# A gather attention kernel: the order of its tiles, the place of a scatter, and an early table load

## The chip, the cores and the metric

The kernel runs on one core of one Trainium2 chip. The metric is the device time of one execution in microseconds (us), lower is better. The core's engines are named as the profile names them: PE is TensorE's matmul stream and PEld its weight loads, DVE is VectorE, ACT is ScalarE, POOL is GpSimd, SP is SyncE. [...]Here POOL issues every indirect DMA (gathers and scatters of rows).

## The reference, cut to what matters

A graph attention layer with a layer norm ahead of it and a residual. N = 3327 nodes, 1024 features. The adjacency matrix is sparse and holds its diagonal; a row has between one and some 37 neighbours.

```python
h = jnp.maximum(_layernorm(x, axis=-1), 0.0)
f = h @ Wf + bf
g = h @ Wg + bg
e = jax.nn.relu(f @ g.T)
scores = jnp.where(adj > 0, e, -9.0e15)
attention = jax.nn.softmax(scores, axis=1)
x = x + attention @ (h @ W + bW)
```

## The kernel before, in words

**First part, 0 to some 258 us.** Rows of `adj` and `x` are read in 26 blocks of 128. For every row the kernel finds its neighbours' numbers (24 in the table `pd`, all candidates in the table `cd`), writes the normalized row to the table `hd`, and builds the product matrix `A_sb` out of Wf and Wg, so that one projection `q = h A` gives what a row is multiplied with. Then it ranks the rows by degree and writes the permutation `perm`.

**Second part, to the end.** The rows in the order of degree make 26 tiles of 128 rows. Tile `s` has `CAPS[s]` slots, one for each neighbour that its fullest row can have: 37, 25, 23, ... down to 11. The list `ORDER` says in which order the tiles are worked on; before, it is 24, 0, 1, ..., 23, 25. For a tile the steps are these:

- `fetch` gathers the neighbour lists `pi` and the tile's own rows (into a buffer `G`) on POOL.
- `prepare` transposes the own rows on PE (`hT`, L703, L704) and makes q on PE in three pieces of 342 columns (`ps_q`, L764); `emptied` and `prepared` copy q out on ACT. Tiles with `s < MORE` (0 and 1) can have more than 24 neighbours: `prepared` gathers their row of `cd` and finds the further numbers on DVE (`found`, `more`, L803 to L812).
- `dot` gathers one neighbour row of each of the 128 rows (512 KB, `G<-hd`, L691) and multiplies it with q on DVE (`junk`, L824).
- `softmax` works on the tile's scores on DVE and ACT.
- `combine` makes the weighted sum of the neighbour rows. A slot is either summed on DVE (`G`, L910), or scaled on ACT (L904) and summed by PE, as eight transposes that add up in `yT_ps` (L887). `on_tensor` chooses how many slots go to PE.
- `project` multiplies the sum with `W_sb` on PE (`ps_o`, L924).
- `result` copies that out on ACT to a tile `res`, and POOL adds the rows of x to it by a gather that accumulates (`res<-in_x_dram`).
- `finish` scatters `res` to the output on POOL (L954).

Tiles with more than 16 slots (`ONE_CHUNK`) are worked on in two units, for example tile 0 as slots 0 to 18 and 19 to 36; smaller ones in one unit, which is then also the last one. The main loop runs over the units. In the last unit of a tile it fetches the tile after next, combines, takes the `result` of the tile before, and prepares the tile after next. `project` of a tile with two-unit successor is put behind the combine of the successor's first unit (`rest`). The first three dots of the next unit (`AHEAD`) are put ahead of `combine`. There are 26 buffers `G`, which all the gathered rows share: a gather waits until the slot that used its buffer has been summed. The tile 24 that comes first has its 12 dots in thirds (`dots_of_first`, L842), and the second tile's gathers stand behind a small POOL copy (`gate`). A list scheduler keeps this order within an engine unless an instruction is not ready by its own estimate; `in_line` pins some of PE's and ACT's instructions to the written order.

Of the kernel before, what the change touches and what calls it, by code (L numbers as in the profile page):

```python
# [8 lines left out]
FP = mybir.dt.float32  # L9
I32 = mybir.dt.int32  # L10
AF = mybir.ActivationFunctionType
# [14 lines left out]

CAPS = [37, 25, 23, 22, 21, 21, 20, 20, 19, 19, 18, 18, 17, 17, 17, 16, 16, 15, 15, 15, 14, 14, 13, 13, 12, 11]

ORDER = [24, *range(24), 25]
ONE_CHUNK = 16  # L30
FIRST = 10
LARGEST = 16
# [263 lines left out]
def edge_path(ctx: ExitStack, tc: tile.TileContext, x, adj, Wf, bf, Wg, bg, W, bW, out, flag):  # L296
# [11 lines left out]
    nc = tc.nc  # L308
    N, D = x.shape
    O = W.shape[1]  # L310
    P = 128
# [26 lines left out]
    ident = const.tile([P, P], FP, name="ident")  # L338
# [345 lines left out]
    small = ctx.enter_context(tc.tile_pool(name="small", bufs=2))  # L684
# [5 lines left out]
    def gather(to, table, idx, **kw):  # L690
        return nc.gpsimd.indirect_dma_start(  # L691
            out=to,
            out_offset=None,
            in_=table,
            in_offset=bass.IndirectOffsetOnAxis(ap=idx, axis=0),
            **kw,
        )
# [13 lines left out]
    @contextmanager  # L711
    def in_line():
        with ExitStack() as both:
            for ins in queue.values():
                both.enter_context(tc.issue_after(ins.ins))
            yield
# [4 lines left out]
    def filled(pool, name, row, w, at):  # L721
        ps = pool.tile([P, CB], FP, name=name)
        if at < 2:
            nc.tensor.matmul(ps, ident, A_sb[:, 0, :CB], start=True, stop=True)
        o = at * w % row.shape[1]
        banks[name, at] = ps
        return nc.scalar.copy(ps[:, :w], row[:, o : o + w])

    for at in range(2):
        filled(p_q, "ps_q", vb, QB, at)  # L730
        filled(p_o, "ps_o", bWb, CB, at)

    def fetch(s):

        if s == ORDER[1]:

            with tc.issue_after(st["gathered"].ins):
                return fetched(s)
        fetched(s)
# [8 lines left out]
    def prepare(s):  # L748
# [9 lines left out]
        for i, o in enumerate(range(0, QW, QB)):  # L758
            at = 3 * ORDER.index(s) + i
            ps = banks.pop(("ps_q", at))  # L760
# [15 lines left out]
    def emptied(s, i):  # L776
        e = st[s]
        at = 3 * ORDER.index(s) + i
        with in_line():
# [37 lines left out]
    def dot(s, k, behind=None):  # L817
        e = st[s]
        g = G[s, k] = gpool.tile([P, D], FP, name="G")
        with tc.issue_after(st["gate"].ins) if s == ORDER[1] else ExitStack():  # L820
            st["gathered"] = gather(g, hd[:, :], e["edges"][k])
# [27 lines left out]
    def softmax(s, k0, k1, last):  # L849

        e = st[s]
        sc = e["sc"][:, k0:k1]
        nc.vector.scalar_tensor_tensor(sc, sc, 0.0, e["mask"][:, k0:k1], op0=ALU.max, op1=ALU.add)
        nm = small.tile([P, 1], FP, name="nm")
        nc.vector.tensor_reduce(nm, sc, AX.X, ALU.max, negate=True)
        if k0:
            nc.vector.tensor_tensor(nm, nm, e["nm"], op=ALU.min)  # L857
        l = small.tile([P, 1], FP, name="l")
        with in_line():
            nc.scalar.activation(sc, sc, AF.Exp, bias=nm, accum_out=l)  # L860
        if k0:
            al = small.tile([P, 1], FP, name="al")
            nc.scalar.activation(al, e["nm"], AF.Exp, bias=nm, scale=-1.0)
            nc.vector.scalar_tensor_tensor(l, e["l"], al, l, op0=ALU.mult, op1=ALU.add)
        if last:
            rs = small.tile([P, 1], FP, name="rs")
            nc.vector.reciprocal(rs, l)
            if k0:
                nc.vector.tensor_tensor(al, al, rs, op=ALU.mult)
            nc.vector.tensor_scalar(sc, sc, rs, None, op0=ALU.mult)  # L870
        if k0:
            queue["act"] = nc.scalar.activation(e["y"], e["y"], AF.Copy, scale=al)
        e["nm"], e["l"] = nm, l

    def on_tensor(s, k0, k1):


        m = min(max(0, CAPS[s] - (7 if s in ORDER[-2:] else 12)), k1 - k0 - 2) if s != ORDER[0] else (k1 - k0) // 2
        ks = range(max(k0, 1), k1)
        return [k for i, k in enumerate(ks) if (i + 1) * m // len(ks) > i * m // len(ks)]  # L880

# [11 lines left out]
    def combine(s, k0, k1, last):  # L893
        e = st[s]
        if not k0:
            e["y"] = G[s, 0]
        y = e["y"]
        e["first"] = True
        pe = on_tensor(s, k0, k1) if last else []
        for k in range(k0, k1):  # L900
            p = e["sc"][:, k : k + 1]
            g = G[s, k]
            if k in pe:
                queue["act"] = nc.scalar.activation(g, g, AF.Copy, scale=p)  # L904
                queue["pe"] = sum_transposed(e, g, e["first"], False)
                e["first"] = False
            elif k == 0:
                queue["act"] = nc.scalar.activation(y, y, AF.Copy, scale=p)  # L908
            else:
                e["summed"] = nc.vector.scalar_tensor_tensor(y, g, p, y, op0=ALU.mult, op1=ALU.add)  # L910

    def project(s):
# [7 lines left out]
        for o in range(OH):  # L920
            ps = banks.pop(("ps_o", OH * ORDER.index(s) + o))
            with in_line():
# [8 lines left out]
    def result(s):  # L931

        e = st[s]
        r = e["r"] = xpool.tile([P, O], FP, name="res")
        for o in range(OH):
            to, ps = r[:, o * CB : (o + 1) * CB], e["o"][o]
            if s == NT - 1:
                nc.vector.tensor_tensor(to, ps, e["x"][:, o * CB : (o + 1) * CB], op=ALU.add)
                continue
            at = OH * ORDER.index(s) + o + 2  # L940
            with in_line():
                ins = nc.scalar.copy(to, ps)  # L942
                if at < OH * NT:
                    ins = filled(p_o, "ps_o", bWb, CB, at)
            queue["act"] = ins


        if s < NT - 1:
            gather(r, x[:, :], perm[:, s : s + 1], compute_op=ALU.add)

    def finish(s):

        with tc.issue_after(st["gathered"].ins):
            ins = nc.gpsimd.indirect_dma_start(  # L954
                out=out[:, :],
                out_offset=bass.IndirectOffsetOnAxis(ap=perm[:, s : s + 1] if s < N // P else final, axis=0),
                in_=st[s]["r"],
                in_offset=None,
                bounds_check=None if s < N // P else N - 1,
                oob_is_err=s < N // P,  # L960
            )
        tc.declare_no_dep(ins.ins, group="results", reason="other rows")
        tc.add_to_no_dep_group("results", ins.ins)

    def failed():

        worst = small.tile([P, 1], FP, name="bad")
        nc.vector.tensor_reduce(worst, bads, AX.X, ALU.max)
        onesf = small.tile([P, 1], FP, name="onesf")
        nc.vector.memset(onesf, 1.0)  # L970
        ps = p_t.tile([P, 4, P], FP, name="ps_t")[:, 0, :]
        nc.tensor.matmul(ps[0:1, 0:1], worst, onesf, start=True, stop=True)
        nc.vector.tensor_copy(flag[0:1, 0:1], ps[0:1, 0:1])
        return nc.values_load(flag[0:1, 0:1], min_val=0, max_val=1 << 20)
# [8 lines left out]
    def dots(s, ks):  # L983
        for k in ks:
            if (s, k) not in done:
                done.add((s, k))

                dot(s, k, st[ORDER[-2]].get("summed") if s == ORDER[-1] else None)
# [13 lines left out]
    rest, done_with = None, []  # L1002
    for i, (s, k0, k1) in enumerate(units):
        last = k1 == CAPS[s]
        at = ORDER.index(s)
        if last and at + 2 < NT:
            fetch(ORDER[at + 2])
        dots(s, range(k0, k1))
        softmax(s, k0, k1, last)
        if i + 1 < len(units):  # L1010
            s2, a, b = units[i + 1]
            dots(s2, range(a, min(b, a + AHEAD)))
        if done_with:
            finish(done_with.pop())
        combine(s, k0, k1, last)
        if rest:
            rest()
            rest = None
        if last:
            if at:  # L1020
                result(ORDER[at - 1])
                done_with.append(ORDER[at - 1])
            if at + 2 < NT:
                prepare(ORDER[at + 2])

            def rest(s=s, at=at):
                if at + 2 < NT:
                    prepared(ORDER[at + 2])
                project(s)

            if not at or i + 1 == len(units) or units[i + 1][2] == CAPS[units[i + 1][0]]:
                rest()
                rest = None
            if at + 2 == NT - 1:
                bad = failed()
# [43 lines left out]
```

## Time and profile before

| | us |
|---|---|
| median of 14 runs | 1326.61 (1323.48 to 1333.57) |
| the profiled execution, its time | 1328.31 |
| its span in the profile | 1326.6 |
| DVE busy | 1165.1 (88%) |
| PE busy | 1110.6 (84%) |
| POOL busy | 893.6 (67%) |
| ACT busy | 597.0 (45%) |

The profiled execution took 1.7 us more than its span, and its time is 1.7 us over the median. A busy share is a mean over stages that have different limits: DVE's 88% hold a first part in which it waits for others, and PE's 84% hold a stretch in which it has nothing to do. The stages have to be read one by one.

### The profile page before, as it was taken

The numbers are of one execution on the slowest core, as the hardware profiler recorded it, in microseconds if no ns is written. First come the engines' busy times: TensorE is split into PE (matmuls) and PEld (weight loads), VectorE is DVE, ScalarE is ACT, GpSimd is POOL, SyncE is SP. The second block draws the span as 40 slices with busy tenths as digits, with TensorE's granted clock in tenths as the row PEclk, the third lists the DMA queues.
The fourth block names the chain that finished last, engine by engine and source line by source line (L and its number), as shares of the span: only waits on it lengthen the run. The fifth ranks groups of instructions, "written<-read, shape, count | busy, mean of one in ns | idle before, by whom it ended". The sixth has DMA issues, their size and how long they took to land.

```text
span 1326.6 us, 14333 instructions
## 1 busy us (share of the span) xinstructions
PE 1110.6 (84%) x4448; PEld 701.4 (53%) x4448; DVE 1165.1 (88%) x2360; ACT 597.0 (45%) x940; POOL 893.6 (67%) x678
## 2 busy tenths in 40 slices
PE   2588897298239679899999998999999999999995
PEld 2355564065035547665665664666566555555553
DVE  4779899769977888999999999999989999998980
ACT  6779688224043516552454454334433333333350
POOL 6699889275656667777776776676656777766611
PEclk9989898699669799999999998999999999999998
DMA  9999996697468788988989889888887899888831
GB/s 357 335 355 378 391 369 219 240 338 293 168 190 301 253 291 272 295 308 301 310 283 327 306 310 320 290 278 296 285 287 233 286 288 291 274 258 295 262 108 50
DMA packets 101660, 374.46 MB, mean 282 GB/s; under 512 B 14731, under 2 KB 18474, under 8 KB 98247
## 3 DMA queue, kind: packets, MB, share of 16 engines
q0 software_dynamic: 79584, 286.77, 64.9%
q1 hardware_dynamic: 11004, 71.01, 14.0%
q10 hardware_dynamic: 10986, 15.67, 3.3%
q8 instruction: 37, 0.61, 0.2%
q14 instruction: 49, 0.40, 0.1%
HBM read 344.11 MB, written 29.30 MB: 281 GB/s over the span
## 4 chain that ended last, share of the span: by engine, by line
PE 29%; DVE 24%; issue 18%; POOL 10%; ACT 9%; DMA 9%; POOLq 0%; ACTq 0%; DVEq 0%; SPq 0%
PE ps_o L924 14%; PE ps_q L764 10%; DVE G L910 7%; ACT G L904 5%; DVE junk L824 5%; DVE cand L478 5%; POOL r L427 5%; DMA G<-hd,pi 5%; POOL G L691 5%; PE yT_ps L887 4%; DMA res<-in_x_dram,perm 2%; DVE junk L842 1%; DVE held L487 1%; DVE cand L489 1%; ACT r L420 1%
## 5 line engine op out<-in xcount | busy, mean ns | idle before, releaser
L691 POOL DMA_INDIRECT G<-hd,pi x454 | 535.0, 1178 | 199.7 <-issue 102.0
L824 DVE CUSTOM_DVE_ANT_0 junk<-G,q 128x1024 bf16<-128x1024 f32 x456 | 584.7, 1282 | 52.9 <-DMA G<-hd,pi 31.2
L924 PE MATMUL ps_o<-W_sb,yT 128*128 128x512 f32 x832 | 367.0, 599 | 21.9 <-ACT yT L918 21.9
L764 PE MATMUL ps_q<-A_sb,hT 128*128 128x342 f32 x1248 | 367.4, 453 | 9.6 <-ACT hT L704 9.6
L910 DVE SCALAR_TENSOR_TENSOR G<-G,sc 128x1024 f32<-128x1024 f32 x279 | 357.8, 1282 | 6.0 <-ACT G L908 5.2
L764 PEld LDWEIGHTS ps_q<-A_sb,hT 128*128 128x128 f32 x1248 | 234.6, 190 | 134.4 <-ACT hT L704 15.8
L924 PEld LDWEIGHTS ps_o<-W_sb,yT 128*128 128x128 f32 x832 | 156.1, 190 | 217.4 <-issue 189.4
L887 PE MATMUL yT_ps<-ident,G 128*128 128x128 f32 x1512 | 186.5, 281 | 78.4 <-ACT G L904 78.4
L887 PEld LDWEIGHTS yT_ps<-ident,G 128*128 128x128 f32 x1512 | 173.8, 144 | 106.5 <-ACT G L904 90.8
L427 POOL TENSOR_TENSOR r<-r,iotaj 128x1664 f32<-128x1664 f32 (+3 forms) x52 | 191.3, 3709 | 29.9 <-ACT r L420 29.9
L904 ACT ACTIVATE G<-G,sc 128x1024 f32<-128x1024 f32 x163 | 173.2, 1136 | 53.1 <-DVE sc L870 53.1
L780 ACT COPY q<-ps_q 128x342 f32<-128x342 f32 x78 | 34.6, 443 | 270.7 <-PE ps_q L764 270.7
L478 DVE MAX8 cand<-r 128x8 f32<-128x208 f32 (+2 forms) x416 | 121.8, 360 | 29.1 <-POOL r L427 29.1
L554 PE MATMUL ps_A<-WgT,WfT 128*128 128x342 f32 x432 | 139.1, 481 | 0.2 <-ACT WfT L535 0.2
L554 PEld LDWEIGHTS ps_A<-WgT,WfT 128*128 128x128 f32 x432 | 85.6, 203 | 59.8 <-issue 19.6
L420 ACT ACTIVATE r<-r 128x3327 f32<-128x3327 int32 (+4 forms) x28 | 77.8, 2780 | 1.4 <-ACT xt L464 0.5
L954 POOL DMA_INDIRECT out_dram<-res,perm x25 | 29.1, 1166 | 65.9 <-DMA res<-in_x_dram,perm 64.4
L860 ACT ACTIVATE sc<-sc,nm 128x10 f32<-128x10 f32 (+11 forms) x41 | 12.6, 308 | 126.4 <-DVE nm L857 115.1
L691 POOL DMA_INDIRECT res<-in_x_dram,perm x25 | 44.4, 1774 | 34.7 <-ACT res L942 29.8
L691 POOL DMA_INDIRECT pi<-pd,perm x26 | 29.9, 1148 | 39.9 <-issue 34.1
L942 ACT COPY res<-ps_o 128x512 f32<-128x512 f32 x50 | 28.7, 575 | 55.8 <-PE ps_o L924 55.8
L704 ACT COPY hT<-ps_t 128x512 f32<-128x512 f32 x52 | 28.0, 587 | 40.2 <-PE ps_t L703 40.1
(133 smaller groups left out, 683.3 us busy)
## 6 DMA issues: line engine op xcount, KB each, us to landing
r<-in_adj_dram SPq DMA_DIRECT2D x25, 1663.5 KB, 10.9
xt<-in_x_dram SPq DMA_DIRECT2D x25, 512.0 KB, 8.6
hd<-xt ACTq DMA_DIRECT2D x25, 512.0 KB, 8.4
G<-hd,pi POOLq DMA_INDIRECT x454, 6.1
wr<-in_L_gnn_Wg_dram SPq DMA_DIRECT2D x8, 512.0 KB, 5.9
wr<-in_L_gnn_Wf_dram SPq DMA_DIRECT2D x8, 512.0 KB, 8.4
W_sb<-in_L_gnn_W_dram SPq DMA_DIRECT2D x1, 4096.0 KB, 17.8
cd<-cand ACTq DMA_DIRECT2D x25, 64.0 KB, 8.5
```

The costliest lines, as they stand in the source:

```text
L420: nc.scalar.activation(r[:n, b:e], a[:n, b:e], AF.Sign, accum_out=to)
L427: nc.gpsimd.tensor_mul(r[:n, b:e], r[:n, b:e], iotaj[:n, : e - b])
L478: nc.vector.max(cand[:n, s * 8 : s * 8 + 8], r[:n, s * SW : min(N, (s + 1) * SW)])
L554: nc.tensor.matmul(ps[:, :QB], WfTs[c][:, k, :], WgT[:, k, o : o + QB], start=(k == 0), stop=(k == KD - 1))
L691: return nc.gpsimd.indirect_dma_start(out=to, out_offset=None, in_=table, in_offset=bass.IndirectOffsetOnAxis(ap=idx, axis=0), **kw,)
L764: ins = nc.tensor.matmul(ps[:, :QB], hT[:, k, :], A_sb[:, k, o : o + QB], start=False, stop=(k == KD - 1), skip_group_check=True,)
L780: ins = nc.scalar.copy(e["q"][:, i * QB : (i + 1) * QB], e["ps_q"][i][:, :QB])
L824: nc.vector.tensor_tensor_reduce(junk, g, e["q"][:, :D], 1.0, e["q"][:, D : D + 1], op0=ALU.mult, op1=ALU.add, accum_out=e["sc"][:, k : k ...
L887: ins = nc.tensor.matmul(e["yT"][:, c, :], g[:, c * P : (c + 1) * P], ident, is_transpose=True, start=(first and c % 4 == 0), stop=(last a ...
L904: queue["act"] = nc.scalar.activation(g, g, AF.Copy, scale=p)
L910: e["summed"] = nc.vector.scalar_tensor_tensor(y, g, p, y, op0=ALU.mult, op1=ALU.add)
L924: ins = nc.tensor.matmul(ps, yT[:, k, :], W_sb[:, k, o * CB : (o + 1) * CB], start=False, stop=(k == KD - 1), skip_group_check=True,)
```

## The change

Four edits. The tile 15, which has 16 slots, moves from the seventeenth place to the second; tile 0 with its 37 slots becomes third, and tile 1 fourth. The rule of `on_tensor` for the first tile (half of the slots on PE) holds for the second one too: 8 slots of tile 15 go to PE, where it was 4. The scatter of a finished tile (`finish`) is issued in the next last unit and no longer in the next unit of any kind; the two differ where a tile has two units. And an exponential of one column is put ahead of the first copies of the second part, so that ACT's exponential table is loaded there.

```diff
-ORDER = [24, *range(24), 25]
+ORDER = [24, 15, *range(15), *range(16, 24), 25]
...
+    one = small.tile([P, 1], FP, name="one")
+    nc.scalar.activation(one, ident[:, :1], AF.Exp)
+
     for at in range(2):
         filled(p_q, "ps_q", vb, QB, at)
         filled(p_o, "ps_o", bWb, CB, at)
...
     def on_tensor(s, k0, k1):
-        m = min(max(0, CAPS[s] - (7 if s in ORDER[-2:] else 12)), k1 - k0 - 2) if s != ORDER[0] else (k1 - k0) // 2
+        m = min(max(0, CAPS[s] - (7 if s in ORDER[-2:] else 12)), k1 - k0 - 2) if s not in ORDER[:2] else (k1 - k0) // 2
...
-        if done_with:
+        if done_with and last:
             finish(done_with.pop())
```

## The prediction

> **What bounds the kernel now.** I read the share by slices first, then the busy time by stretches of 40 us, then the chain of work that ended last, then the timeline around the places that the change touches. The second part starts at 258 us, and the slices say that its limit changes on the way:
>
> ```profile
> PE   2588897298239679899999998999999999999995
> DVE  4779899769977888999999999999989999998980
> ```
>
> PE has its hole at slice 11 (around 350 us) and is full from about slice 25; DVE is nearly full between. The stretches give numbers (columns: stretch, length, busy PE, PEld, DVE, ACT, POOL with counts, PE clock, DMA share, GB/s):
>
> ```profile
> 300.00:340.00 40.00, 36.21 (x144) 21.89 (x144) 38.72 (x56) 13.89 (x22) 18.42 (x18) 1.00 0.62 229
> 340.00:380.00 40.00, 0.00 (x0) 0.00 (x0) 36.80 (x49) 0.00 (x0) 26.83 (x16) 0.52 0.61 198
> 460.00:500.00 40.00, 31.02 (x103) 17.71 (x102) 32.58 (x49) 10.95 (x22) 27.49 (x23) 0.94 0.85 288
> 620.00:660.00 40.00, 35.90 (x161) 22.95 (x160) 39.65 (x62) 19.43 (x30) 29.04 (x26) 1.00 0.90 304
> 1020.00:1060.00 40.00, 39.09 (x149) 24.09 (x148) 39.37 (x55) 13.51 (x23) 29.90 (x24) 1.00 0.92 303
> ```
>
> From 340 to 380 us PE does nothing: it has made q and o for all that is ready, and tile 0's 37 slots occupy DVE until 384. From 386 to some 620 us both have gaps, to 960 us DVE is the limit, and from there the chain of waits lies on PE without a break:
>
> ```profile
> 1029.24 14.00 PE ps_o L924 x32
> 1043.24 3.49 PE yT_ps L887 x32
> 1047.85 14.08 PE ps_q L764 x48
> 1063.47 14.00 PE ps_o L924 x32
> ```
>
> So the early tiles cost DVE time, the late ones PE time. The third view is the timeline at the first scatter and at the table load:
>
> ```profile
> 405.83 1.59 POOL L691 DMA_INDIRECT res<-in_x_dram,perm  x1 [0.30 <-issue]
> 409.35 1.02 POOL L691 DMA_INDIRECT G<-hd,pi  x1 [0.30 <-issue]
> 414.49 0.99 POOL L954 DMA_INDIRECT out_dram<-res,perm  x1 [4.12 <-DMA res<-in_x_dram,perm]
> 415.73 1.32 DVE L824 CUSTOM_DVE_ANT_0 junk<-G,q 128x1024 bf16<-128x1024 f32 x1 [4.73 <-DMA G<-hd,pi]
> 415.79 0.97 POOL L691 DMA_INDIRECT G<-hd,pi  x1 [0.30 <-issue]
> 421.29 1.28 DVE L824 CUSTOM_DVE_ANT_0 junk<-G,q 128x1024 bf16<-128x1024 f32 x1 [0.39 <-DMA G<-hd,pi]
> ...
> 295.38 1.28 ACT L860 ACT_TABLE_LOAD   x1
> 298.36 0.17 DVE L855 TENSOR_REDUCE nm<-sc 128x1 f32<-128x12 f32 x1
> 298.56 0.30 ACT L860 ACTIVATE sc<-sc,nm 128x12 f32<-128x12 f32 x1 [1.90 <-DVE nm L855]
> ```
>
> The scatter holds POOL 4.1 us, but whom does that hurt? Counting gathers against dots in order, the dot at 415.73 uses the gather of 407.73, issued before the scatter: its row landed late behind the accumulating gather `res`. The first row behind the scatter is that of 415.79, and its dot waits 0.39 us.
>
> **What the skill says.** The Trainium skill, SBUF — State Buffer, section "SBUF: two separate sides", has DVE instructions with two SBUF inputs and GpSimd share a port as an exclusive lock. The trace agrees: a gather's issue takes 0.94 us alone and 1.75 us between sums. ScalarE: Activation LUTs, section "What ACT_TABLE_LOAD costs", gives some 1283 ns for a load; the trace has 1.28. DMA: Bandwidth & Descriptors, section "SWDGE vs HWDGE vs iDMA", says that GpSimd's DMAs have one queue of descriptors; the trace shows the consequence, a row gather behind `res` landing after 8.0 us where its neighbours take 5.5.
>
> **The parts and their cost.**
>
> *Tile 15 second, late side.* From its o at 1029.24 to the next at 1063.47 the tile holds PE for 34.2 us: o 14.0, q 14.1, five times eight transposes some 4.4, hT about 1, the rest gaps. All is on the path there, and all its POOL work (16 row gathers, lists, own rows, `res`, scatter), its DVE work (16 dots, 11 sums) and ACT work leave with it: **minus 34.2**. The neighbours stay PE-bound: tile 14's successor brings DVE about the same, 16 slots.
>
> *Tile 15 second, early side.* PE takes it for nothing: between 339 us and tile 0's combine (386.6) it idles 47 us, and what tile 15 puts there is about 40 us (the next q, its o, 72 transposes). POOL stands still for 5.7 and 10.0 us before 337. So DVE pays. It makes 16 dots and 7 sums more (15 sums without the first slot, 8 of them on PE). Seven pairs of a sum and a dot at 2.40 us (two of the 1.20 steps seen from 337 to 366) are 16.8; nine lone dots at 1.33 are 12.0; mask and softmax about 1.0. Tile 1's `found` and `more` move too: now in DVE's idle first stage (293 to 296 us), they come in tile 0's dots, where DVE is full: 3 x 0.29 + 2 x 0.37 + 0.22, with overlap 1.6; tile 0's take their place in the idle stage, and its `cd` gather is behind, not ahead of the first row gathers. Lists and own rows of tile 1 are gathered before tile 15's fourth row; they move rows by 2.5 us that have 6 or more to spare. **Plus 31.4**.
>
> *Are the rows there?* 16 rows of tile 15 and 12 of tile 24 exceed the 26 buffers as 37 and 12 do now. The new danger is after tile 15's combine: its buffers come free from about 334, DVE runs seven pairs to about 350 and then nine lone dots. With gathers at the 1.3 to 2.4 us steps seen here I count eight rows issued ahead by then, enough but for **0.5**; bounds 0 and 3. Tile 1's `more` waits 3.2 us for tile 0's gathers now (L812 at 370.33); it may wait less, so minus 3.2 is a bound below.
>
> *Half of its sums on PE.* Counted above; without it four more sums, 4.4 to 4.8 us, would be on DVE. Four scalings (1.14 us) lie on ACT, idle from 334 to 381; four times eight transposes (1.04 each) in PE's hole.
>
> *Scatter in last units.* Tiles 0 to 14 and the first one. POOL's waits before L954 sum to 64.4 us, yet only the dots whose gather is issued behind a scatter count: 0.39, 0.43, 0.27 and 2.11 us (at 421, 478, 571, 612), in all 3.2. Later scatters wait as well, and DVE has 8 to 15 us of rows in hand. In its new place, after the third dot of the next tile, the scatter meets a landed `res`, so it costs only its 1.3 us of POOL and half a megabyte in the queue. From tile 1 on the rows are 12 us ahead there, free; at tile 0 they arrive 6 us after issue with no reserve, and DVE loses about 1.0. **Minus 2.2**; bounds minus 5 (the wait's knock-on to later rows) and plus 3 (each scatter hurts).
>
> *Exponential table.* ACT's load at 295.38 ends at 296.66 and the exponential waits for DVE to 298.5, so nothing is gained: **0**. It goes to an ACT that is idle until 261 for want of `bWb`; if this cover failed, hT's copy at 266.04 would be up to 1.5 late.
>
> Sum: 31.4 + 0.5 - 34.2 - 2.2 = **-4.5**. On the profiled execution, 1328.3 us (span 1326.6), that is 1323.8; that execution is 1.7 over the median of the runs, so I expect a median of **1322.1**.
>
> **The rivals.** (1) *Rows run short in the second tile*, slower. If gathers keep the 2.40 us step of the buffer-bound stretch (1.75 issue, 0.65 wait) while DVE goes at 1.33, nine lone dots lose up to 9 x 1.07 = 9.6: -4.5 + 9.6, or 1331.7. It decides as soon as fewer than four rows lie ready when the lone dots begin (9 x (1 - 1.33/2.40) = 4). For it speaks that exactly this happened after tile 0's combine (waits of 3.1, 1.0, 0.6, 0.5, 2.2 us after 388); against it, that only 8 and not 16 slots wait for PE. (2) *The scatter was the cause of all five waits.* Then 4.73 + 4.46 + 3.05 + 2.00 + 2.11 = 16.4 go instead of 3.2: 1309. For it: each stands right at a scatter; against: the order of gathers. (3) *A wash*: the moved tile costs DVE early what it saves late, because the list scheduler puts a wait of some 4 us elsewhere: 1326 or a little more.
>
> **How the numbers follow.** My forecast gets 0.55 (0.45 of it faster than the bound, 0.10 within), rival 2 0.17, rival 1 0.20, rival 3 0.08 (0.03 within, 0.05 slower). The bound of what can be told from no change is 0.2%, 2.7 us. Faster 0.62, same 0.13, slower 0.25. The forecast's own range, from the bounds, is 1314 to 1328. The full range takes in most of both rivals: 1311 to 1331.
>
> **What would show it.** Right: PE's empty stretch shrinks to under 40 us; tile 0's exponential of 18 slots moves from 381.6 to about 413; the chain is on PE from about 990; the waits before L954 go from 64 us to some 25, while waits of 2 to 4 us at dots behind `res` stay. Wrong: waits for rows at 350 to 365 of over 5 us (rival 1), or no wait at a dot behind `res` at all (rival 2). The forecast as a whole fails if PE is not the limit after tile 14, for then the late tile does not give back its 34 us.

## The result, and the profile after

The changed kernel takes 1316.95 us (median of 10 runs, 1315.48 to 1320.07); the kernel before takes 1327.58 (median of 47 runs). The ratio is 0.9921, with a 95% interval from 0.9907 to 0.9935: faster by 10.5 us, with 8.6 and 12.3 as ends. The profiled execution of the changed kernel takes 1316.06 us with a span of 1314.3, so between the two profiled executions lie 12.3 us.

The slices of the page, busy share in tenths:

```profile
PE   2598896288952968999999999899999999999995
DVE  3779998859998888899999999999998999999980
```

The hole of PE has moved to the right by one slice, 33 us. Three stretches of 40 us, with the columns that the prediction used:

```profile
340.00:380.00 40.00, 36.47 (x161) 23.71 (x160) 39.11 (x61) 12.07 (x21) 27.87 (x25) 1.00 0.84 281
380.00:420.00 40.00, 5.03 (x18) 3.24 (x18) 39.23 (x59) 5.31 (x8) 22.60 (x15) 0.59 0.62 205
460.00:500.00 40.00, 29.92 (x159) 23.01 (x158) 31.26 (x55) 20.99 (x29) 27.73 (x23) 0.87 0.78 253
```

Tile 15 fills 340 to 380; PE then has only 5 us of work from 380 to 420, while DVE is full with tile 0. From 460 on DVE still has gaps: 31.3 of 40 us busy, 32.6 before. The chain of waits lies on PE to the end, from 981.86 on:

```profile
981.86 14.00 PE ps_o L929 x32
995.86 4.37 PE yT_ps L892 x40
1001.34 14.08 PE ps_q L769 x48
1016.95 14.00 PE ps_o L929 x32
1030.95 3.49 PE yT_ps L892 x32
1035.56 14.08 PE ps_q L769 x48
1051.18 14.00 PE ps_o L929 x32
```

The o that starts at 1016.95 is tile 14's, the next is tile 16's. Before, they started at 995.02 and 1063.47, with tile 15's between them. Of the signs that the prediction named, PE's empty stretch is now 35.0 us (under 40 was named), tile 0's exponential of 18 slots starts at 411.34 (some 413), and the waits ahead of the scatters sum to 31.6 us (some 25).

Laid side by side the two profiles give this account (L870 before and L875 after mark the end of a tile's softmax):

| stretch | before | after | difference | forecast |
|---|---|---|---|---|
| start to the first tile's exponential (12 slots) | 298.6 | 300.6 | +2.1 | 0 |
| from there to tile 0's softmax end (18 slots) | 85.7 | 114.5 | +28.8 | +31.9 |
| from there to tile 14's softmax end | 582.7 | 573.8 | -8.9 | -2.2 |
| from there to the end | 359.6 | 325.4 | -34.3 | -34.2 |

The last row came out to 0.1 us, the second 3 us under the forecast. The first and the third need the experiments. Two more views of the changed kernel prepare them. The first is ScalarE's timeline, where the load of the table is:

```profile
0.81 1.28 ACT L732 ACT_TABLE_LOAD   x1 [0.81 <-PEq L1072]
2.10 0.20 ACT L732 ACTIVATE one<-ident 128x1 f32<-128x1 f32 x1
15.41 1.28 ACT L455 ACT_TABLE_LOAD   x1
297.91 1.28 ACT L865 ACT_TABLE_LOAD   x1
300.64 0.30 ACT L865 ACTIVATE sc<-sc,nm 128x12 f32<-128x12 f32 x1 [1.44 <-DVE nm L860]
```

The early exponential waits for nothing but `ident`, so the list scheduler took it to 2.1 us. At 15.41 the square root's table replaces it, and the load at 298 is still there. **The edit does not do what it says.** The second view is the timeline around the first `res` after tile 0, and the scatter that belongs to it:

```profile
435.14 1.60 POOL L692 DMA_INDIRECT res<-in_x_dram,perm  x1 [1.85 <-ACT res L947]
437.05 1.30 POOL L692 DMA_INDIRECT G<-hd,pi  x1 [0.30 <-issue]
438.65 1.00 POOL L692 DMA_INDIRECT G<-hd,pi  x1 [0.30 <-issue]
439.96 1.01 POOL L692 DMA_INDIRECT G<-hd,pi  x1 [0.30 <-issue]
444.19 1.28 DVE L829 CUSTOM_DVE_ANT_0 junk<-G,q 128x1024 bf16<-128x1024 f32 x1 [4.02 <-DMA G<-hd,pi]
...
456.37 0.99 POOL L959 DMA_INDIRECT out_dram<-res,perm  x1 [0.30 <-issue]
```

POOL now issues gathers straight on behind `res`, where before the scatter's wait of 4.12 us held back the gather behind it until 415.79; the scatter comes 21 us after `res` and waits for nothing. The dot at 444.19 uses the gather of 437.05, the first behind `res`, and waits 4.02 us all the same. In the page's groups (busy us, mean ns, idle time before, what ended most of it) the scatter's wait fell from 64.4 us to this (what is left comes after 800 us, at tiles of one unit):

```profile
L959 POOL DMA_INDIRECT out_dram<-res,perm x25 | 29.3, 1171 | 35.7 <-DMA res<-in_x_dram,perm 31.6
```

### The profile page after: what moved, and what is told of

Read it like the earlier page. It is cut to its first block, busy times and chain, and to the rows that moved or that the text cites. A ratio compares the mean times of both kernels' runs of the same rounds, so it can differ in the third digit from the quotient of the medians.

```text
span 1314.3 us, 14404 instructions
## 1 busy us (share of the span) xinstructions
PE 1110.6 (85%) x4480; PEld 703.6 (54%) x4480; DVE 1159.6 (88%) x2356; ACT 600.7 (46%) x945; POOL 893.8 (68%) x678
## 4 chain that ended last, share of the span: by engine, by line
PE 32%; DVE 21%; issue 15%; DMA 12%; POOL 10%; ACT 9%; POOLq 0%; ACTq 0%; DVEq 0%; SPq 0%
PE ps_o L929 15%; PE ps_q L769 12%; DVE G L915 8%; DMA G<-hd,pi 7%; POOL r L428 6%; ACT G L909 5%; DVE junk L829 5%; POOL G L692 4%; PE yT_ps L892 4%; DVE cand L479 3%; DMA xt<-in_x_dram 1%; DMA hd<-xt 1%; DVE junk L847 1%; PE ps_A L555 1%; DVE sc L829 1%
## 5 line engine op out<-in xcount | busy, mean ns | idle before, releaser
L829 DVE CUSTOM_DVE_ANT_0 junk<-G,q 128x1024 bf16<-128x1024 f32 x456 | 584.6, 1282 | 46.6 <-DMA G<-hd,pi 25.1
L915 DVE SCALAR_TENSOR_TENSOR G<-G,sc 128x1024 f32<-128x1024 f32 x275 | 352.7, 1283 | 4.3 <-ACT G L913 3.6
L892 PE MATMUL yT_ps<-ident,G 128*128 128x128 f32 x1544 | 191.4, 282 | 58.0 <-ACT G L909 58.0
L892 PEld LDWEIGHTS yT_ps<-ident,G 128*128 128x128 f32 x1544 | 178.9, 145 | 85.8 <-ACT G L909 69.5
L909 ACT ACTIVATE G<-G,sc 128x1024 f32<-128x1024 f32 x167 | 177.6, 1137 | 65.7 <-DVE sc L875 65.7
L959 POOL DMA_INDIRECT out_dram<-res,perm x25 | 29.3, 1171 | 35.7 <-DMA res<-in_x_dram,perm 31.6
```

The source lines that it names most:

```text
L829: nc.vector.tensor_tensor_reduce(junk, g, e["q"][:, :D], 1.0, e["q"][:, D : D + 1], op0=ALU.mult, op1=ALU.add, accum_out=e["sc"][:, k : k ...
L892: ins = nc.tensor.matmul(e["yT"][:, c, :], g[:, c * P : (c + 1) * P], ident, is_transpose=True, start=(first and c % 4 == 0), stop=(last a ...
```

## The experiments

**First set: the edits apart.** The four kernels ran on one chip, beside the kernel before (1326.36 us).

The scatter alone, on the kernel before:

```diff
-        if done_with:
+        if done_with and last:
             finish(done_with.pop())
```

> The kernel before, with the scatter in last units only and nothing else. Prediction as written: only the dots whose gather is issued behind a scatter count, so 2 us faster (ratio 0.998). Theory A, from the comparison of the two traces (from tile 0's softmax to tile 14's the changed kernel is 8.9 us shorter): the scatter's wait delays all the later gathers and costs more than its own dots show, so 7 to 9 us faster (0.993 to 0.995). Rival 2, all five waits were the scatter's: 16 us faster (0.988), with no wait left at a dot behind res.

Measured: 1321.09 us, ratio 0.9961 (0.9949 to 0.9974), 5.2 us faster (3.4 to 6.8). That is over the prediction's 2 us, just under theory A's 7 to 9, and a third of rival 2's.

The changed kernel with the scatter put back:

> The changed kernel with the scatter back in the next unit of any kind; the new order, the half on TensorE and the early table stay. Prediction as written: 2.3 us faster than before (0.998). Theory A: 3 to 5 us faster than before (0.996 to 0.998), since in the trace tile 0's softmax moved by 28.8 us beyond the start of the second part and the late part gave back 34.2. Rival 2: 6 us slower than before.

Measured: 1322.76 us, ratio 0.9977 (0.9966 to 0.9988), 3.0 us faster than before, within theory A's range and near the prediction's 2.3. Rival 2 had it slower and is out. Against the changed kernel's ratio the scatter is worth 0.9977 - 0.9921, or 7.4 us here, with some 2.4 either way, and 5.2 alone; the intervals of the two overlap.

The early exponential alone:

> The kernel before with the early exponential alone. Prediction and theory A: the table load was hidden before and is hidden after, no change (within 0.2%), if the load is moved at all. Rival: the load delays the first copies of the second part and with them the first tile, 1.3 us slower.

Measured: 1327.61 us, ratio 1.001 (0.9998 to 1.0022): no gain, and 1.3 us slower, with 0.3 faster and 2.9 slower as ends. The size fits the rival, but not its reason: the profile has the exponential at 2.1 us and a load at 296.5, as the changed kernel has, so no load stands ahead of the first copies.

Half of the sums on TensorE taken back:

```diff
-... if s not in ORDER[:2] else (k1 - k0) // 2
+... if s != ORDER[0] else (k1 - k0) // 2
```

> The changed kernel with only 4 instead of 8 slots of tile 15 summed on TensorE (the old rule); the rest as changed. Prediction: four more sums on VectorE ahead of tile 0's softmax, 4.4 to 4.8 us slower than the changed kernel, so about 6 us faster than before (0.9955). Rival: the sums run where VectorE would wait for rows anyway, no difference to the changed kernel (0.992).

Measured: 1323.17 us, ratio 0.9982 (0.9969 to 0.9995), so 8 us slower than the changed kernel by the two ratios, with some 2.5 us either way. The stretch from the first exponential to tile 0's softmax end is 119.8 us in its profile, against 114.5 (changed kernel) and 113.7 (scatter put back): four sums cost 5.3 to 6.1 us there, a little more than the forecast's 4.8. The other 2 to 3 us are not explained; in the one profile the stretch from tile 0 to tile 14 is 2.4 us longer than the changed kernel's. The rival, no difference, is out.

Six profiles of these kernels allow a count over tiles 0 to 14: each wait of a dot for its row, put down to `res` or to a scatter if one of them is among the three DMAs that POOL issued ahead of its gather (to the later one of the two). Waits of over 0.15 us count, in us:

| kernel | scatter | stretch, tile 0 to 14 | DVE idle in it | behind scatter | behind res | others |
|---|---|---|---|---|---|---|
| before | any unit | 582.7 | 32.5 | 3.4 | 14.5 | 13.2 |
| early exponential alone | any unit | 583.3 | 32.8 | 6.0 | 12.9 | 13.9 |
| changed, scatter put back | any unit | 579.6 | 29.9 | 4.7 | 12.9 | 12.4 |
| scatter alone | last unit | 572.2 | 23.6 | 0 | 11.2 | 12.4 |
| changed | last unit | 573.8 | 25.1 | 0 | 13.2 | 12.0 |
| changed, 4 sums on PE | last unit | 576.2 | 27.6 | 0.3 | 12.8 | 14.5 |

Only one column of waits goes away with the scatter's move, and it is the one that the prediction named: the dots behind a scatter, 4.7 us in the mean. What waits behind `res` stays at 11 to 15 us. DVE's whole idle time falls from 31.7 to 25.4 us in the mean, by 6.3, and the medians say 5.2 and 7.4. Each row is a single execution, and they were not equally typical: the profiled ones of the upper three kernels took 0.6 us more than the medians of their runs in the mean, those of the lower three 2.0 us less (5.1 for the scatter alone). So the profiles flatter the scatter's move by some 2.7 us; the column behind the scatter does not rest on that, since it falls to 0 to 0.3 in all three.

**Second and third set: the table load, and the bounds.** The second set of four ran on another chip, the third on the first chip again. In both the kernel before takes 1349 to 1350 us, and the profiles show waits of ScalarE whose end the profile puts down to "remote": 19 to 62 us in sum in each, none in the six profiles above. The name is misleading. Every one of these waits stands at a copy of what TensorE has just made (`hT`, `q`, `yT`, once `res`) and is for TensorE's semaphore (one of them for POOL's too). In the run `a_nores2` below, for example:

```profile
626.48 1.04 PE L704 MATMUL ps_t<-ident,G 128*128 128x128 f32 x8
630.71 0.59 ACT L705 COPY hT<-ps_t 128x512 f32<-128x512 f32 x1 [2.99 <-remote]
631.35 3.31 PE L769 MATMUL ps_q<-A_sb,hT 128*128 128x342 f32 x6 [3.83 <-issue]
```

By the profile, which models the ends of matmuls, the transposes are over at 627.52, but the copy of them starts at 630.71. So TensorE's results came some microseconds later in these sets than the profile has them. It shows no instruction that accounts for the delay, and its cause stays open; that it lies outside the kernel is not shown. The ratios to before have wide intervals, and small differences can't be read from them. They also shift between sets: the changed kernel itself has 0.9921 in the result above and 0.9868 in the third set.

The exponential left out of the changed kernel, twice:

> The changed kernel without the early exponential. In the traces the exponential runs at 2.1 us, its table is replaced at 15.4, and the load at 297.9 is still there; the four profiled kernels that have the edit begin their first softmax (exponential of 12 slots) at 299.8 to 300.6 us, the two without it at 298.0 and 298.6. Theory A: the edit moves no load, it only disturbs the order of the first part, which costs some 2 us: 2 us faster than the changed kernel, 0.9905 of before. Rival (the prediction): it is free and useless, 0.992.

> The changed kernel without the early exponential, once more beside the changed kernel itself. Theory A: the edit only disturbs the order of the first part, 1 to 2 us: 0.9905 to 0.991. Rival (the prediction): free and useless, 0.992. In the profile the first softmax then begins 1 to 2 us earlier than in the changed kernel.

Measured: 0.9915 (0.9889 to 0.9941), and 0.990 (0.9833 to 0.9966) beside 0.9868 (0.9823 to 0.9914) for the changed kernel itself. That settles nothing. For a small cost of the edit speak the profiles of the first set and the two of before and after: the first tile's exponential comes at 300.4, 300.5, 300.6 and 299.8 us in the four kernels that have the edit and at 298.6 and 298.0 in the two without. The order of the first part's instructions on DVE and ACT differs between the kernel before and the one with only this edit, and by the third block of rows the scan for neighbours is 1.8 us behind (43.46 against 41.63). The later sets don't bear it out evenly: in the third the exponential comes at 303.4 and 300.1 us with the edit and at 298.5 and 298.8 without, but in the second, leaving out `a_lateexp`, at 300.6 with it and at 302.5 and 302.4 without. A cost of 1 to 2 us is thus likely, not shown in the times.

The exponential tied behind the first copies, so that the load falls where it was meant to be:

```diff
-    one = small.tile([P, 1], FP, name="one")
-    nc.scalar.activation(one, ident[:, :1], AF.Exp)
...
-        filled(p_o, "ps_o", bWb, CB, at)
+        ins = filled(p_o, "ps_o", bWb, CB, at)
+
+    one = small.tile([P, 1], FP, name="one")
+    with tc.issue_after(ins.ins):
+        nc.scalar.activation(one, ident[:, :1], AF.Exp)
```

> The changed kernel with the exponential tied behind the last of the first copies on ScalarE, so that the load comes at about 265 us, where the change meant it to be. Prediction and theory A: no load at 297, and nothing gained by that, since the exponential of the first tile waits for VectorE anyway: same as the changed kernel without the edit (0.9905). Rival: the first tile's chain gets shorter by the load's 1.3 us (0.9895).

Measured: 0.9912 (0.9879 to 0.9944), beside 0.9915 without any exponential in the same set. Lines of its timeline:

```profile
264.66 1.11 ACT L728 COPY ps_o<-bWb 128x512 f32<-128x512 f32 x2 [8.44 <-DMA bWb<-in_L_gnn_bW_dram]
265.77 1.28 ACT L737 ACT_TABLE_LOAD   x1
267.07 0.20 ACT L737 ACTIVATE one<-ident 128x1 f32<-128x1 f32 x1
...
301.79 0.17 DVE L861 TENSOR_REDUCE nm<-sc 128x1 f32<-128x12 f32 x1
301.99 0.30 ACT L866 ACTIVATE sc<-sc,nm 128x12 f32<-128x12 f32 x1 [3.38 <-issue]
```

Now the load is in the idle time, none is left at 298, and ScalarE sits idle for 3.38 us ahead of the first tile's exponential where it sat 1.90 before. The profile calls the end of this wait "issue", but the operand `nm` is finished at 301.96. The load was hidden, and taking it away made the wait longer by about as much. No gain shows in the time, within the width of the interval.

The scatters left out:

```diff
         if done_with:
-            finish(done_with.pop())
+            s0 = done_with.pop()
+            if ORDER.index(s0) > 14:
+                finish(s0)
```

> The kernel before with the scatters of the first fifteen tiles in order left out (their rows of the output are not written). It is the bound for the scatter's whole cost: its wait, its issue and half a megabyte each. Moving them was worth 5.2 us. Theory A, the wait of GpSimd was the cost and the new place is free: 5 to 6 us faster than before (0.9955 to 0.996). Rival, the new place still costs (issue and bytes in the stretch that is short of rows): 9 to 13 us faster (0.990 to 0.993).

Measured: 1333.11 us, ratio 0.988 (0.9851 to 0.9909), more than either theory gave, though the interval reaches into the rival's range. Read plainly, a scatter that is moved still costs something. But the 0.9961 of the moved scatter is from another set, and the stretch of this profile from tile 0 to tile 14 takes 583 us, a wait of 7.7 us for ScalarE among them, no less than in the kernel before in its undisturbed profile, so the profile doesn't say where the gain lies. What the scatters cost in their new place stays open.

The accumulating gather left out, twice:

```diff
-        if s < NT - 1:
+        if s < NT - 1 and ORDER.index(s) > 15:
             gather(r, x[:, :], perm[:, s : s + 1], compute_op=ALU.add)
```

> The changed kernel without the accumulating gather of x in the first sixteen tiles of the order (the residual is left out there). Prediction: the waits at dots right behind res (4.0, 3.8, 4.5 and 0.9 us in the changed kernel's trace, 13.2 in all) are that gather's, and go: 9 to 13 us faster than the changed kernel (0.982 to 0.985 of before). Rival: those dots wait because the buffers came free late; without res the waits stay, 0 to 3 us (0.990 to 0.992).

> The changed kernel without the accumulating gather of x in the first sixteen tiles of the order (the residual is left out there), once more. In the first run of it the waits behind res were gone, but ScalarE stood still for up to 9.7 us for causes outside the program, so its time tells little. Prediction: the 13.2 us of waits behind res go and most of it is gained, 0.982 to 0.986. Rival: VectorE then waits at the same places for ScalarE's first scaling, which stands behind the copies of q, and little is gained: 0.989 to 0.992.

Measured: 0.9938 (0.991 to 0.9965) and 0.9916 (0.988 to 0.9952); nothing is gained. Part of the prediction's reading holds: no dot waits behind `res` any more. The count is 0 by its own rule once `res` is gone, but the other waits of dots didn't take its place: 11.2 and 11.3 us in the two profiles, where the changed kernel has 12.0 beside 13.2 behind `res`, and 13.4 beside 13.5 in the third set. But DVE waits anew, as the rival said, at the first sum of a tile:

```profile
596.10 0.45 ACT L785 COPY q<-ps_q 128x342 f32<-128x342 f32 x1 [7.95 <-remote]
596.58 0.45 ACT L728 COPY ps_q<-vb 128x342 f32<-128x342 f32 x1
596.96 0.30 ACT L865 ACTIVATE sc<-sc,nm 128x10 f32<-128x10 f32 x1
597.38 1.15 ACT L913 ACTIVATE G<-G,sc 128x1024 f32<-128x1024 f32 x1
598.56 1.28 DVE L915 SCALAR_TENSOR_TENSOR G<-G,sc 128x1024 f32<-128x1024 f32 x1 [4.75 <-ACT G L913]
```

The exponential and the first scaling stand on ScalarE behind the copy of q (596.10), and that copy waited for TensorE's late q. Such waits of 2.2 to 5.7 us come at seven tiles in a row from 507 to 773. How much of them is the order on ScalarE and how much TensorE's lateness can't be told from these runs; whether the 13 us behind `res` are to be had stays open.

One step on in the order, without the exponential:

```diff
-ORDER = [24, 15, *range(15), *range(16, 24), 25]
+ORDER = [24, 15, 16, *range(15), *range(17, 24), 25]
...
-... if s not in ORDER[:2] else (k1 - k0) // 2
+... if s not in ORDER[:3] else (k1 - k0) // 2
```

> The changed kernel once more, as the yardstick for the three that run beside it: 0.992 of before, as measured.

> The order goes one step on: tiles 24, 15, 16, then 0; half of the slots of 15 and of 16 on TensorE; without the early exponential. By the prediction's own working a further tile of 16 slots costs VectorE 16 dots and 7 sums more ahead of tile 0 (seven pairs at 2.40, nine dots at 1.33, 1.0: 29.8 us) and gives back 34.2 on TensorE late: 4.4 us faster than without this step, 0.987 of before. Rival: TensorE's empty stretch ahead of tile 0's combine is 38 us now, and 40 more don't fit, or rows run short before tile 0: no gain or a loss, 0.991 to 0.994.

Measured: the changed kernel 0.9868 (0.9823 to 0.9914), the step further 0.9896 (0.9843 to 0.9949). No gain is shown, and the changed kernel remains the best one measured. In the profile of the step further, tile 16's exponential follows tile 15's by 35.2 us (334.41 to 369.62), where 29.8 were worked out; waits of 1.60, 0.99 and 2.22 us are in it. At 35.2 the step costs what the late side pays back: from tile 14's softmax end to the end the profile has 292.2 us, against 326.4 for the changed kernel in the same set. So the late side repeats to the forecast's 34.2, and the waits, 4.8 us in sum, eat the gain; the 2.22 are for ScalarE's copy of q, so part of them can be this set's.

## Why the prediction was right, and where it was not

**Direction and range** were right: faster, 1316.95 us within 1311 to 1331. The size was low: 10.5 us measured, 4.5 forecast. By its steps:

*Late side of tile 15: right.* -34.2 forecast, -34.3 in the profiles. The chain is on PE from 982 (some 990 forecast), the condition under which the late tile gives back all of its TensorE time.

*Early side: right, and 3 us too dear.* +31.9 forecast, +28.8 measured. The bound that was named below it came true: tile 1's `more` waited 3.20 us for tile 0's gathers before and 0.74 after. No row was missing in the lone dots of tile 0 (the 0.5), and apart from these 0.74 us no wait over 0.57 us stands between 303 and 400: rival 1 fell. Taken together with the late side the order is worth some 5 us, and the kernel with the scatter put back shows 3.0 with the exponential's likely 1 to 2 against it.

*Half of the sums: right in kind*, 5.3 to 6.1 us on DVE instead of 4.4 to 4.8, and some 8 in the time.

*Scatter: the term that was mis-sized.* The step "only the dots whose gather is issued behind a scatter count: 0.39, 0.43, 0.27 and 2.11 us (at 421, 478, 571, 612), in all 3.2", less 1.0 for the new place, gave -2.2. Measured are -5.2 alone and -7.4 on top of the order. The mechanism stands in the table above: exactly those waits went, and those behind `res` stayed, which is against rival 2. Three things made the sum small. It came from one execution whose waits behind scatters are the lowest of three (3.4 with one of 0.16 that was left out; 6.0 and 4.7 in the others). The 1.0 for the place before tile 0's combine did not come: behind scatters the waits are 0 to 0.3 in the new place. And DVE's other idle time fell by a further 1.7 in the mean (6.3 less 4.6), of which 1.0 stood behind `res`; that is within what the choice of executions does, so it is not shown to be the scatter's. The 4.6 lie within the interval of the 5.2, and just under that of the 7.4 (5.0 to 9.8); what is over stays open.

*Exponential table: the number right, the step wrong.* "It goes to an ACT that is idle until 261" was not so; the instruction went to 2.1 us and moved no load. That nothing was to be gained was right for the reason given: with the load truly moved, ScalarE only waited longer for DVE.

## What to carry to other kernels

Where a kernel has a stretch bound by one engine and a later one bound by another, an item of work that is moved between them is paid at the price of the engine that is full where it arrives and paid back at that of the engine that is full where it left; here 28.8 for 34.3 us. When an in-order queue stands still on a wait, match the requests behind it with the instructions that need them before charging the wait, and count over several executions, since such waits differ between them (here 3.4 to 6.0 us behind scatters). And under a list scheduler look up in the trace where an instruction went: one that depends on nothing goes to the front, and can disturb an order that it has nothing to do with.

## What the runs showed of the hardware

A row gather right behind an accumulating gather of 512 KB lands late. Over tiles 0 to 14 of the six profiles in the table of waits the median from issue to landing is 7.0 to 7.5 us for it, and 6.0 to 6.1 for the rows that don't follow `res`. At the first three such gathers of each profile, where rows are short, the dot waits 2.2 to 4.7 us, wherever the scatter stands; from the fifth on DVE has rows in hand, and it waits 0.7 us or less. Leaving `res` out took these waits away. The prediction calls this a consequence of GpSimd's one queue; that the queue is the cause, and not the bytes of `res`, no run shows.

The prediction's 0.94 and 1.75 us for a gather's issue have a simple rule behind them. Four lines of the kernel before:

```profile
304.37 1.28 DVE L910 SCALAR_TENSOR_TENSOR G<-G,sc 128x1024 f32<-128x1024 f32 x1
304.37 0.95 POOL L691 DMA_INDIRECT G<-hd,pi  x1 [0.30 <-PE yT_ps L887]
337.02 1.28 DVE L824 CUSTOM_DVE_ANT_0 junk<-G,q 128x1024 bf16<-128x1024 f32 x1
337.37 1.75 POOL L691 DMA_INDIRECT G<-hd,more  x1 [10.03 <-DVE G L910]
```

The gather that starts together with a sum takes 0.95 us; the one that starts 0.35 us into a dot takes 1.75. All 140 row gathers in this profile whose issue takes over 1.3 us, and all 137 in the changed kernel's, end 0.81 to 0.87 us after the end of the dot or sum in which they began. So it isn't the sums that make an issue long, but beginning in the middle of either.

And one chip gave the same kernel 1326 us in the first set and 1350 in the third. The granted clock of the kernel before was 0.940 in the median of the first set, 0.931 and 0.929 in the other two, and TensorE's results came late there, as shown above. The changed kernel's two profiles put the loss of 18.0 us at 2.8, 5.9, 8.3 and 1.0 us in the four stretches of the first table, so hardly into the last, which is bound by PE. In these sets the 95% interval of a ratio grew from 0.0025 to between 0.005 and 0.013, in the third set in part because fewer runs were made.
